# Reordering the beginning, the output projections of the last image, and the last stores of a convolution-attention kernel

## The chip, the core and the metric

The kernel runs on one core of a Trainium2 chip. A core has a matrix engine (TensorE, PE in the profile), a vector engine (VectorE, DVE), an activation engine (ScalarE, ACT), a general engine (GpSimd, POOL) and a synchronizing engine (SyncE, SP). Each takes its instructions in the order in which the program gives them to it. SP, ACT and POOL also issue DMA transfers from their queues. The metric is the device time of one execution in microseconds (us); the time before is the median of five runs.

## The reference

The input x is (4 images, 384 channels, 48 x 48). Cut to what matters:

```python
local = conv7x7_depthwise(x, conv_w)                # one 7x7 filter per channel
local = local * inv + (bn_beta - bn_mean * inv)     # inv = bn_gamma * rsqrt(bn_var + eps)
x_norm = layernorm(x_flat)                          # over the 384 channels, per pixel
q, k, v = split(x_norm @ qkv_w.T + qkv_b)           # 8 heads of 48
q = q + layernorm(local_flat)
attn = softmax((q @ k.T) * 48 ** -0.5)              # per image and head, 2304 x 2304
out = x_flat + (attn @ v) @ proj_w.T + proj_b
```

## The kernel before

**Tiles.** Channels lie on the partitions, three chunks of 128. Pixels are worked in groups of 384 (8 rows of 48), six per image, 24 in all; `t` counts them. For each image the keys and values of all six groups are made first (`from_x`); then the groups pass through attention, twelve slots each. A slot `s` is `scores` (12 products of keys and queries of one head pair, into PSUM, with ACT taking exponentials) followed by `weigh` of the slot before (24 matmul instructions with the values). PSUM has three places of two banks each, called the ring (`r`), one bank `m` that `bank()` hands out, and one bank `o` for the attention sums. A new `bank()` has to wait until everybody has read the old one.

**The convolution** is 49 taps x 3 chunks = 147 instructions of DVE per group, `acc += weight * shifted x` (L239 for a chunk's first tap, L243 for the others). `taps` is sorted by the row shift and then the column shift. `conv_ops` yields after each instruction, and `stream` chains all groups. For t = 0, chunk 0, the first ten taps (`PE_TAPS`) are done by PE as products with diagonal matrices (`make_diagonals` on ACT, `first_products`), added later by `add_products` (L761); `acc` of that chunk starts at zero (L229). So group 0 has 137 instructions on DVE.

**What sets the order.** PE, DVE and ACT run in the order written in the program, as do SP and POOL for the first loads. In the beginning `convolve_first(n)` places n taps by hand. In the slots a planner does it: `spare` estimates the time that DVE has in each half of a slot, `due` says that the taps of group t must be done by slot 6 of group t-1 (slot 8 of t = 0), and `plan` spreads the taps over the halves, starting from those already done. `convolve("slot", t, s, half)` takes them.

**The beginning.** The normalization of a group (`Norm`) is: mean over the channels, by PE, with a matrix of 1/384 (`mean_of` with three matmuls on the three chunks, or `sum` on DVE at L352 and L353 and then `mean`, one matmul, at L364); `centre` on DVE (L372); `squares` on ACT (L349); sum and mean again; `root` on ACT (L377 to L379); `newton` on DVE (L384 to L386); `scale` (L441). `newton` reads the bank `m` too.

The weights of the projections are scaled by the layer norm's gain on ACT: `scale_values` (L551), and `scale_rows(i, c)` (L558, L559) for keys (i = 1) and queries (i = 0). The layer norm's shift goes through the unscaled weights into a row for each of queries (0), keys (1) and values (2): `shift_rows` has PE multiply the shift with the weights, `rows_out` has ACT copy the row to SBUF and issue a DMA to DRAM (`bias`), and POOL issues four DMAs that bring it back as columns. `key_bias` (L562, L563) and `query_bias` (L567, L568) add these columns on DVE; ACT needs the sums when it moves keys and queries out of PSUM (L481, L494). The loads are on SP's queue in this order: the slab for the convolution, x of group 0, value weights, key weights, query weights, x of group 1, x of groups 2 to 5.

`from_x` yields after each pair of projections: two value blocks; the third value block and key 0; keys 1 and 2; queries 0 and 1; query 2. Of the first image all six groups are normalized in one loop, in which the norm of group g+1 is placed between the projections of group g; in the last turn it is the norm of the local values of group 0. `local_end` and `query_end` then add these to the queries.

**The outputs.** For images 0 to 2 the attention's results are kept in DRAM and projected in the next image's `from_x`. In the last image, group t-1 is projected in slots 5, 8 and 10 of group t, one chunk at a time in `m` (`output_step`), and `finish` (L700) adds bias and x on DVE and stores from SP (L703). `spare` lowers and raises the planner's time in these slots.

**The end.** `judge[0]` counts on PE the sums outside a safe range; `judge[1]` makes a flag of it on DVE (L1029, L1030). All engines load that flag (L1033) and branch (L1034): a second pass with shifted exponents would follow, and is skipped here.

Of the kernel before, what the change touches and what calls it, by code (L numbers as in the profile page):

```python
# [12 lines left out]
ALU = mybir.AluOpType  # L13
# [14 lines left out]
OUT_SLOTS = 5, 8, 10  # L28
PE_TAPS = 10

# [13 lines left out]
def unshifted_pass(  # L44
# [138 lines left out]
    load_packed(staged[1], qkv_wT[:, C : 2 * C])  # L183
    load_packed(staged[0], qkv_wT[:, 0:C])
    load_x(0, 1)
# [35 lines left out]
    def conv_ops(t):  # L221
# [9 lines left out]
        for i, tap in enumerate(taps):  # L231
            for c in range(CC) if t or i >= PE_TAPS else range(1, CC):
                part = window(slab, acc[:, c, :], g, first, end, c, tap)
                if not part:
                    continue
                src, dst = part
                weight = cw[:, c, tap : tap + 1]
                if tap == taps[0]:
                    nc.vector.tensor_scalar(  # L239
                        dst, src, weight, shift[:, c : c + 1], ALU.mult, ALU.add  # L240
                    )
                else:
                    nc.vector.scalar_tensor_tensor(dst, src, weight, dst, ALU.mult, ALU.add)  # L243
                yield
# [27 lines left out]
    def spare(t, s, half):  # L272
# [7 lines left out]
        if g:  # L280
            time -= {(2, 0): 0.7, (4, 1): 1.4}.get((s, half), 0.0)
            if b == B - 1 and s in OUT_SLOTS:
                time += -0.6 if half else 2.1
# [239 lines left out]
    def shift_rows(some):  # L523
        r = ring() if len(some) > 1 else None
        for j, i in enumerate(some):
            rows[i] = bank()[0:1, :C] if r is None else r[0:1, j, :C]
            project(
                rows[i],
                lambda c: beta[:, c : c + 1],
                lambda c: staged[i][:, c, :] if i < 2 else w_v[:, c, :],  # L530
            )
# [159 lines left out]
    def output_step(t, co):  # L691
        ao = outputs[t][0]
        m = bank()
        project(m[:, :G], lambda c: w_o[:, c, co * P : (co + 1) * P], lambda c: ao[:, c, :])
        finish(t, co, m[:, :G])

    def finish(t, co, m):
# [5 lines left out]
        nc.sync.dma_start(  # L703
# [61 lines left out]
    convolve_first(2)  # L765
    norm = Norm(xn[0, 0])
    norm.mean_of(norm.src)
    first_products(1)
    shift_rows((2, 1))
    convolve_first(4)  # L770
    norm.centre()
    norm.squares()
    columns = rows_out((1, 2))
    convolve_first(4)
    norm.mean_of(norm.buf)
    norm.root()
    shift_rows((0,))
    first_products(6)
    scale_values()
    columns_q = rows_out((0,))  # L780
    convolve_first(4)
    norm.scale(norm.newton())
    for c in range(CC):
        scale_rows(1, c)
    for g in range(NG):
# [4 lines left out]
        if g == 0:  # L790
            scale_rows(0, 0)
        convolve_first(10 if last else 4)
        if g == 0:
            add_products()
        norm = Norm(accs[0] if last else xn[0, g + 1])
        norm.sum()
        if g == 0:
            key_bias(columns)
        if last:
            next(making)  # L800
        norm.mean()
        convolve_first(3)
# [3 lines left out]
        if g == 0:  # L806
            scale_rows(0, 1)
            scale_rows(0, 2)
# [3 lines left out]
        norm.root()  # L812
        next(making)
        if g == 0:
            query_bias(columns_q)
        next(making)
        next(making, None)
        convolve_first(5 if last else 13)
        if last:
            local_end(0, norm.newton())  # L820
            query_end(0)
        else:
            norm.scale(norm.newton())
    plan(n_first - (each - PE_TAPS))

    for t in range(NT):
# [51 lines left out]
        for s in range(NSLOT):  # L878
# [47 lines left out]
            if s in OUT_SLOTS and g and not next_image:  # L926
                output_step(t - 1, OUT_SLOTS.index(s))
# [613 lines left out]
```

## Time and profile before

| | |
|---|---|
| median of five runs | 2972.28 us (2969.0 to 2972.81) |
| the profiled execution | 2969.26 us, span 2967.1 us |
| PE busy | 2942.5 us (99%) |
| DVE busy | 2308.5 us (78%) |
| ACT busy | 1562.9 us (53%) |
| first matmul starts | 10.94 us |
| first value projection starts | 32.43 us |
| scores of group 0 start | 147.39 us |
| last matmul ends | 2959.2 us |
| mean granted clock of PE | 0.998 |

How the lines are read. A timeline's line has the start in us, the duration in us, the engine, the line of the kernel, the operation, what it writes and reads (partitions x elements), how often, and in brackets how long the engine was idle before and what ended that. A matmul of float32 shows as two instructions. A queue has a `q` behind the engine's name. A line of the list of waits has the engine and line that waited, what for, the sum in us, how often, and the longest. A line of the table by stretches has the stretch, its length, the busy time and count of PE, its weight loads, DVE, ACT and POOL, then the clock granted to PE (1.00 is full), the DMA share and GB/s.

### The profile page before, as it was taken

What the parts mean: (1) busy time and instruction counts of PE and PEld (TensorE: products, weight loads), DVE (VectorE), ACT (ScalarE), POOL (GpSimd) and SP (SyncE); (2) the same over time, 40 slices, a digit from 0 to 9 for tenths busy, and PEclk for the clock granted to TensorE, in tenths of its full rate; (3) what the DMA queues carried; (4) which work ended last, traced back from release to release, by engine and by line L of the source; (5) the groups of instructions that cost most, each with busy time, mean ns of one, the idle gap of its engine ahead of it and who ended that gap; (6) DMA issues with size and microseconds to landing.
All of it is one profiled execution on the core that took longest, in us unless ns stands there. A gap on an engine that the chain in (4) does not pass through costs nothing.

```text
span 2967.1 us, 42344 instructions
## 1 busy us (share of the span) xinstructions
PE 2942.5 (99%) x15658; PEld 1358.0 (46%) x15658; DVE 2308.5 (78%) x4574; ACT 1562.9 (53%) x2365; POOL 25.0 (1%) x71
## 2 busy tenths in 40 slices
PE   8999999999999999999999999999999999999998
PEld 4544444444554444444455444444455444444443
DVE  7899999898788787877788878787778867677311
ACT  4355666565225565665523655566542465555553
POOL 2000000000000000000000000000000000000000
PEclk9999999999999999999999999999999999999999
DMA  6101111201231111111132111102113210100001
GB/s 111 31 13 25 44 39 32 43 22 33 83 86 24 29 34 30 30 35 35 24 90 74 26 36 33 33 21 43 37 38 91 50 26 16 33 27 20 17 26 30
DMA packets 102189, 116.53 MB, mean 39 GB/s; under 512 B 43330, under 2 KB 88915, under 8 KB 101972
## 3 DMA queue, kind: packets, MB, share of 16 engines
q1 hardware_dynamic: 100512, 113.56, 16.3%
q8 instruction: 125, 2.05, 0.3%
q14 instruction: 92, 0.75, 0.1%
q0 software_dynamic: 960, 0.07, 0.0%
q10 hardware_dynamic: 500, 0.11, 0.0%
HBM read 79.03 MB, written 24.09 MB: 35 GB/s over the span
## 4 chain that ended last, share of the span: by engine, by line
PE 96%; DVE 3%; DMA 0%; ACT 0%; issue 0%; ACTq 0%; SPq 0%; DVEq 0%
PE r L722 39%; PE o L737 38%; PE r L446 17%; DVE acc L243 3%; PE m L446 1%; PE m L364 0%; PE r L975 0%; DMA staged<-in_qkv_wT_dram 0%; DMA taps_in<-in_conv_w_dram 0%; DVE xn L372 0%; PE o L261 0%; DMA vec<-natural 0%; DVE sq L352 0%; DVE sq L353 0%; ACTq L165 0%
## 5 line engine op out<-in xcount | busy, mean ns | idle before, releaser
L726 ACT ACTIVATE pt<-r 128x768 f32<-128x768 f32 x1728 | 1275.9, 812 | 969.1 <-PE o L737 490.3
L243 DVE SCALAR_TENSOR_TENSOR acc<-slab,vec,acc 128x368 f32<-128x368 f32 (+5 forms) x3447 | 1747.3, 582 | 0.0
L737 PE MATMUL o<-pt,v 128*49 128x384 f32 x6912 | 1177.2, 490 | 0.1
L722 PE MATMUL r<-xn,k 48*128 48x384 f32 x5184 | 908.7, 497 | 0.0
L737 PEld LDWEIGHTS o<-pt,v 128*49 128x49 f32 x6912 | 426.7, 124 | 711.4 <-issue 664.4
L722 PEld LDWEIGHTS r<-xn,k 48*128 48x128 f32 x5184 | 438.3, 185 | 469.4 <-ACT pt L726 232.1
L722 PE MATMUL r<-qt,kt 48*128 48x384 f32 x1728 | 300.4, 494 | 0.0
L446 PE MATMUL r<-xn,w_qk 128*128 128x384 f32 x864 | 283.7, 486 | 0.0
L722 PEld LDWEIGHTS r<-qt,kt 48*128 48x128 f32 x1728 | 149.8, 185 | 150.3 <-ACT pt L726 68.8
L446 PEld LDWEIGHTS r<-xn,w_qk 128*128 128x128 f32 x864 | 164.2, 190 | 114.5
L352 DVE TENSOR_TENSOR sq<-sq 128x384 f32<-128x384 f32 x47 | 26.1, 555 | 163.6 <-ACT sq L349 163.5
L446 PE MATMUL r<-w_v,xn 128*128 128x384 f32 x432 | 144.4, 487 | 0.0
L643 DVE RECIPROCAL rd<-rd 128x24 f32<-128x24 f32 (+2 forms) x25 | 7.5, 301 | 168.6 <-DMA rd<-den 168.4
L475 ACT COPY v<-r 128x384 f32<-128x384 f32 x72 | 32.1, 481 | 200.3 <-PE r L446 200.3
L446 PEld LDWEIGHTS r<-w_v,xn 128*128 128x128 f32 x432 | 81.8, 190 | 58.2 <-issue 1.8
L700 DVE SCALAR_TENSOR_TENSOR xr<-r,pb,xr 128x384 f32<-128x384 f32 x57 | 33.3, 612 | 90.2 <-ACT xn L494 84.3
L494 ACT ACTIVATE xn<-r,qkb 128x384 f32<-128x384 f32 x72 | 41.8, 580 | 99.4 <-PE r L446 97.4
L446 PE MATMUL r<-af,w_o 128*128 128x384 f32 x270 | 89.5, 486 | 0.0
L481 ACT ACTIVATE k<-r,qkb 128x384 f32<-128x384 f32 x72 | 39.3, 580 | 57.4 <-PE r L446 57.4
L446 PEld LDWEIGHTS r<-af,w_o 128*128 128x128 f32 x270 | 51.3, 190 | 35.8
L626 ACT COPY ao<-o 49x384 f32<-49x384 f32 x141 | 66.7, 473 | 1.7
L700 DVE SCALAR_TENSOR_TENSOR xr<-m,pb,xr 128x384 f32<-128x384 f32 x15 | 9.2, 616 | 60.1 <-PE m L446 60.1
(117 smaller groups left out, 824.0 us busy)
## 6 DMA issues: line engine op xcount, KB each, us to landing
xr<-in_x_dram SPq DMA_DIRECT2D x24, 576.0 KB
out_dram<-xr SPq DMA_DIRECT2D x72, 192.0 KB
slab<-in_x_dram SPq DMA_DIRECT2D x32, 378.0 KB
xn<-in_x_dram SPq DMA_DIRECT2D x48, 216.0 KB
rb<-rden SPq DMA_DIRECT2D x48, 216.0 KB
held<-ao SPq DMA_DIRECT2D x15, 576.0 KB
af<-held SPq DMA_DIRECT2D x15, 576.0 KB
slab<-in_x_dram SPq DMA_DIRECT2D x16, 297.0 KB
```

Source lines behind the costliest of these rows:

```text
L243: nc.vector.scalar_tensor_tensor(dst, src, weight, dst, ALU.mult, ALU.add)
L352: nc.vector.tensor_add(self.buf[:, 0, :], src[:, 0, :], src[:, 1, :])
L446: nc.tensor.matmul(dst, lhsT=weights(c), rhs=src(c), start=c == 0, stop=c == CC - 1)
L475: nc.scalar.copy(v[:, blk, :, 0:HD], r[:, :C].rearrange("p (h d) -> p h d", d=HD))
L481: nc.scalar.activation(k[:, u, :], r[:, :G], AF.Identity, bias=qkb[:, 1, u : u + 1])
L494: nc.scalar.activation(src[:, i, :], q[:, :G], AF.Identity, bias=qkb[:, 0, i : i + 1])
L626: nc.scalar.copy(dst[r : r + HA], sums[r : r + HA, :G])
L643: nc.vector.reciprocal(rd, rd)
L700: nc.vector.scalar_tensor_tensor(xr[:, co, :], m, pb[:, co : co + 1], xr[:, co, :], ALU.add, ALU.add)
L722: nc.tensor.matmul(r[:, j, :G], lhsT=kk[:, blk * P : (blk + 1) * P], rhs=qq, start=True, stop=True)
L726: nc.scalar.activation(pt, r[:, :, :G], AF.Exp, scale=SCALE)
L737: nc.tensor.matmul(sums[r : r + HA, :G], lhsT=values[t // NG, kb // NB][:, kb % NB, 2 * p + j, :], rhs=pt[:, j, :], start=kb == 0, stop=kb ...
```

## The change

Four things move; no arithmetic is added or dropped.

1. The beginning. DVE's first eight instructions are now taps 10 to 17 of chunk 0, then the chunks 1 and 2 in turn, then the rest of chunk 0. The first mean of x is issued before those taps, after three products. The rows are made one at a time: values, then keys behind the mean of the squares, then queries in the first turn of the loop, behind the projection of value 2 and key 0; this last one uses bank `m`, and its copy, its DMAs and the scaling of the query weights come behind it. On SP, x of group 1 is loaded before the query weights.
2. The loop. All six turns have the same order: four taps, sum, mean, five taps, centring, three taps, sum of squares, thirteen taps (eight in the last turn), with the query projections after the scaling. In the first turn `add_products` and `key_bias` stand between the mean and the five taps. 165 taps are issued before the planner begins, where it was 150.
3. The last image's outputs. All three chunks are projected in a row in slot 5, behind the weighing and the taps of that slot's second half, into two places of the ring; the planner's estimate changes with it.
4. The end. The flag is made before the first `finish`, and the second store is issued by ACT.

```diff
-OUT_SLOTS = 5, 8, 10
+OUT_SLOT = 5
+AHEAD = 8
...
+    load_x(0, 1)
     load_packed(staged[0], qkv_wT[:, 0:C])
-    load_x(0, 1)
...
+        order = [(tap, c) for tap in taps for c in range(CC)]
+        if t == 0:
+            mine = [(tap, 0) for tap in taps[PE_TAPS:]]
+            order = mine[:AHEAD] + [o for o in order if o[1]] + mine[AHEAD:]
+        for tap, c in order:
...
-            if b == B - 1 and s in OUT_SLOTS:
-                time += -0.6 if half else 2.1
+            if b == B - 1 and s == OUT_SLOT and half:
+                time += 5.8 - 1.9
...
-    def shift_rows(some):
-        r = ring() if len(some) > 1 else None
-        for j, i in enumerate(some):
-            rows[i] = bank()[0:1, :C] if r is None else r[0:1, j, :C]
+    def shift_row(i, place):
+        rows[i] = place[0:1, :C]
...
-    def output_step(t, co):
+    def output(t):
         ao = outputs[t][0]
-        m = bank()
-        project(m[:, :G], lambda c: w_o[:, c, co * P : (co + 1) * P], lambda c: ao[:, c, :])
-        finish(t, co, m[:, :G])
-
-    def finish(t, co, m):
+        r, r2 = ring(), ring()
+        for co, m in enumerate((r[:, 0, :G], r[:, 1, :G], r2[:, 0, :G])):
+            project(m, lambda c: w_o[:, c, co * P : (co + 1) * P], lambda c: ao[:, c, :])
+            finish(t, co, m)
+
+    def finish(t, co, m, queue=nc.sync):
...
     first_products(3)
-    convolve_first(2)
     norm = Norm(xn[0, 0])
     norm.mean_of(norm.src)
-    first_products(1)
-    shift_rows((2, 1))
-    convolve_first(4)
+    convolve_first(AHEAD)
     norm.centre()
     norm.squares()
-    columns = rows_out((1, 2))
-    convolve_first(4)
+    first_products(3)
+    r = ring()
+    shift_row(2, r[:, 0, :])
+    scale_values()
+    convolve_first(12)
     norm.mean_of(norm.buf)
     norm.root()
-    shift_rows((0,))
-    first_products(6)
-    scale_values()
-    columns_q = rows_out((0,))
-    convolve_first(4)
-    norm.scale(norm.newton())
+    shift_row(1, r[:, 1, :])
+    first_products(4)
+    columns = rows_out((1, 2))
     for c in range(CC):
         scale_rows(1, c)
+    norm.scale(norm.newton())
     for g in range(NG):
         last = g == NG - 1
         making = from_x(0, g)
         next(making)
-        if g == 0:
-            scale_rows(0, 0)
-        convolve_first(10 if last else 4)
+        convolve_first(4)
+        norm = Norm(accs[0] if last else xn[0, g + 1])
+        norm.sum()
+        norm.mean()
         if g == 0:
             add_products()
-        norm = Norm(accs[0] if last else xn[0, g + 1])
-        norm.sum()
-        if g == 0:
             key_bias(columns)
-        if last:
-            next(making)
-        norm.mean()
-        convolve_first(3)
+        convolve_first(5)
         norm.centre()
         norm.squares()
         next(making)
         if g == 0:
-            scale_rows(0, 1)
-            scale_rows(0, 2)
+            shift_row(0, bank())
+            columns = rows_out((0,))
         convolve_first(3)
         norm.sum_squares()
         norm.mean()
         norm.root()
+        if g == 0:
+            for c in range(CC):
+                scale_rows(0, c)
         next(making)
-        if g == 0:
-            query_bias(columns_q)
-        next(making)
-        next(making, None)
-        convolve_first(5 if last else 13)
+        convolve_first(8 if last else 13)
         if last:
             local_end(0, norm.newton())
-            query_end(0)
         else:
             norm.scale(norm.newton())
+        if g == 0:
+            query_bias(columns)
+        next(making)
+        next(making)
+    query_end(0)
...
-            if s in OUT_SLOTS and g and not next_image:
-                output_step(t - 1, OUT_SLOTS.index(s))
...
             convolve("slot", t, s, 1)
+            if s == OUT_SLOT and g and not next_image:
+                output(t - 1)
...
+    judge[1]()
     finish(NT - 1, 0, parts[0])
-    judge[1]()
-    finish(NT - 1, 1, parts[1])
+    finish(NT - 1, 1, parts[1], nc.scalar)
     finish(NT - 1, 2, parts[2])
```

## The prediction

> **What bounds the kernel now.** I read the page's busy shares first, then the list of what TensorE (PE) waited for, then the timelines of PE, VectorE (DVE), ScalarE (ACT) and the queues in the first 60 us, around 217 us, in the last image and at the end.
>
> ```profile
> PE 2942.5 (99%) x15658; PEld 1358.0 (46%) x15658; DVE 2308.5 (78%) x4574; ACT 1562.9 (53%) x2365; POOL 25.0 (1%) x71
> ```
> PE works for 2942.5 of 2967.1 us. Its 24.6 us of idle time, plus time in which it runs slowly, are all that a change of order can win. The waits of PE say where they are:
>
> ```profile
> PE o L261 <- ACT pt L251: 10.9, 1, 10.9
> PE m L446 <- DVE sq L384: 2.5, 1, 2.5
> PE m L364 <- DVE sq L353: 2.5, 4, 1.7
> PE r L446 <- DMA staged<-in_qkv_wT_dram: 0.3, 1, 0.3
> ```
> The first 10.9 us are the way to the first weights, which the change leaves alone. The last matmul ends at 2959.2, about 7.9 us before the span does. Between them lie three places. Place 1 is the query row, held back until DVE has read the one bank `m`:
>
> ```profile
> 26.70 2.10 PE L446 MATMUL m<-staged,vec 128*1 128x384 f32 x6 [2.49 <-DVE sq L384]
> 32.43 4.03 PE L446 MATMUL r<-w_v,xn 128*128 128x384 f32 x12
> ```
> Place 2 is the first mean of local values in group 0, for which DVE's taps are late:
>
> ```profile
> 218.43 0.91 PE L364 MATMUL m<-sq,mean_w 128*128 128x384 f32 x2 [1.66 <-DVE sq L353]
> 219.28 5.77 PE L737 MATMUL o<-pt,v 128*49 128x384 f32 x24
> ...
> 229.14 4.08 PE L737 MATMUL o<-pt,v 128*49 128x384 f32 x24
> ```
> Behind the stall the same 24 matmuls take 5.77 us, not 4.08. The stretches of that time show why: the granted clock (the column after POOL) falls to half.
>
> ```profile
> 219.00:221.00 2.00, 2.00 (x10) 0.72 (x10) 2.00 (x5) 0.52 (x1) 0.00 (x0) 0.69 1.06 200
> 221.00:223.00 2.00, 2.00 (x10) 0.68 (x8) 2.00 (x4) 1.10 (x2) 0.00 (x0) 0.50 1.04 174
> ```
> Place 3 is the last image, where each output projection stands alone between scores and weighing:
>
> ```profile
> 2466.09 4.21 PE L722 MATMUL r<-xn,k 48*128 48x384 f32 x24
> 2470.23 2.20 PE L446 MATMUL m<-ao,w_o 128*128 128x384 f32 x6
> 2472.36 4.08 PE L737 MATMUL o<-pt,v 128*49 128x384 f32 x24
> ```
>
> **Part 1, the beginning.** No matmul goes or comes, so the question is what PE waits for. Times from the span's start. The way to 14.89 stays (three products at the slow initial pace). Then: mean of x, to 16.9; three products at 0.65, 18.9; value row 2.0, 20.8; mean of squares 2.0, 22.8; key row 2.0, 24.85; four products 2.6, 27.4. DVE does its eight taps (0.52 each, 34.37 row: 1.50 for three) from about 10.5 to 14.7, waits, centres at 17.05 to 18.4 (before: 17.99), squares end on ACT at 19.6, twelve taps end at 24.5. ACT: value weights 20.9 to 22.5 (1.61), root 22.9 to 24.65 (0.58+0.52+0.52 with starts). Newton and scale, 3.2 us (26.03 to 29.23 before), end at 27.85. The first value projection starts at 27.9, not 32.43: a gain of 4.5, of which 2.1 are only the query row, moved behind. The net 2.4 is the idle time taken out (0.32+2.49, less 0.5 that PE waits for the scale).
>
> Now what is queued behind `key_bias` on DVE. Its columns go through DRAM, and this path starts later:
>
> ```profile
> 22.11 0.88 ACT L539 COPY row<-r 1x384 f32<-1x384 f32 x2 [1.58 <-PE r L446]
> 23.03 0.49 ACTq L544 DMA_DIRECT2D bias<-row  x1
> 27.11 2.19 POOL L98 DMA_DIRECT2D columns<-bias  x4 [6.83 <-DMA bias<-row]
> 34.23 0.15 DVE L562 TENSOR_TENSOR qkb<-qk_vec,columns 128x3 f32<-128x3 f32 x1
> ```
> The fourth of POOL's issues, at 28.75, took 4.0 to land, so row issue to columns is 9.7 us, and before they were there (32.75) when DVE came (34.23). Now the key row ends at 24.85, the copies take 0.92, the issue is at 25.8 and the columns land at 35.5. DVE comes after four taps (2.1), the sum (1.1) and the added products (0.6) at 31.6: a new wait of 3.9. Behind it stand five taps (2.55) and the centring (1.3), which frees bank `m` at 39.7. PE has done values, mean, value 2 and key 0 (27.9+3.9+0.7+3.9) at 36.4 and wants that bank for the moved query row: idle 3.3. The row ends at 41.75; ACT (squares, two copies, row copy) frees `m` at 42.3, DVE's sums are ready then too, and the mean of squares starts at 42.3, where before it was 41.17: +1.1. The row before the stall of 217 us says that 1.66 us of idling cost the clock as well (5.77-4.08 = 1.7); the 2.49 us at 24 us did not (the next 2.10 is full speed). I take a slow stretch, partly under waits: +1.1 more; bounds 0 and 1.7.
>
> The query row's own chain: row copy 0.47, ACT issue 0.22, four POOL issues and a landing, 10.0 us in all (29.33 to 39.3 before), so columns at 52 to 53.5, where DVE arrives at 51.9: up to 1.6 of wait. Its twelve weight scalings (3.3) now follow the root, to 48.3 to 49.5, and query 0 needs the last third of them at 48.5 to 49.7: at nothing. SP: x of group 1 is issued four DMAs (about 2 us) earlier, the query weights as much later, wanted only at 39.7; the later x tiles are behind the bias row as before (SP waited 3.8 and 3.9 for it). From 42.3 DVE then needs thirteen taps 6.45, newton and scale 3.15, the wait 0.5, bias and four taps 2.3, sum 1.1, five taps 2.45, centring 1.3, three taps 1.5, sums 1.1: group 1's mean of squares starts at 62.1, 1.9 late (60.22 before), and 3.0 late with the slow clock. In later groups five taps instead of three add 1.0 on DVE before the centring; DVE waited 1.6, 2.0 and 2.0 there, so they are covered, in group 1 (0.98) just. If that cover were gone, each group would lose up to 1.0. Part 1: **+2.7**, the 3.0 less what PE's own small waits of the later groups before (0.1 to 0.3 each) give back; bounds -2.4 (DVE doesn't wait, the net gain above) and +4.5 (1.7 of clock, and 1.0 in one group).
>
> A page would price the wait otherwise. "DMA: Bandwidth & Descriptors" of the Trainium skill, section Anatomy of one DMA, gives about 2.0 us fixed for a small DMA. By that, as an estimate, the two hops save 3.5 and Part 1 would be about -1.6; the trace has 3.5 to 4.2 for each hop, and I go by it.
>
> **Part 2, group 0.** 165 taps are issued in the beginning, not 150. The planner's formula, worked out for both starts (13 and 28 done), gives slots 0 to 7 126 taps instead of 134. At 0.515 (69.0 us for 134) that is 64.9, and 1.1 for the sum. The query end is at DVE about 1.6 us before scores begin (before: 0.8 after), as eight taps, newton and two ends fit into five projections. So the sum is ready 64.4 us after scores begin, PE asks at 69.4 (216.77-147.39). The stall goes, and with it the slow clock: -1.66-1.7 = **-3.35**; bounds -3.4 and 0. Late next is nothing that I find: the second mean has 2 us more than it used. The Trainium skill, "TensorE: Matmul & The Clock Gate", HAM oscillation, warns only of idle gaps above about 3.4 us; by that this gap costs no clock, and Part 2 would be -1.66. The rows at 0.50 decide.
>
> **Part 3, outputs.** Alone, a projection takes 2.13 (2470.23 to 2472.36), three 6.39. Eighteen in a row behind weighing take 5.9 (742.16 to 748.07). Saved: 0.45 in each of five groups, **-2.2**; bounds -2.7 and 0. The cover: two of three ring buffers are held until `finish`. DVE sat idle 6.97 before its output at 2472.47, and the six extra taps take 3.2 of it; then finish 2 ends 0.7 before scores want its buffer. Without that cover the loss is what DVE is late, per group. The sum behind moves 7 us, but waits for ACT's squares two slots on anyway (5.83).
>
> **Part 4, the end.** The flag's two instructions (0.33) go into DVE's 1.52 of idling, the last finish and its issue come 0.3 earlier; ACT takes one issue. PE's branch (4.6 us) starts up to 1.3 earlier, SP's 0.35: **-0.5**; bounds -1.3 and 0.
>
> **Sum.** +2.7-3.35-2.2-0.5 = -3.4 (rounded). The profiled execution took 2969.26 us, 2.2 beyond its span; it would take 2965.9. The median of the runs, 2972.28, is 3.0 above it, so the forecast is 2968.9. A measurement here tells about 0.2% (5.9 us) from no change, so this is no change. Its own range is 2966 (Part 1 at 1.0, the others at their lower bounds: -6.4) to 2973 (Part 1 at 4.5, Part 3 at half: -0.4, and one more for the others).
>
> **Rivals.** *The beginning wins* (0.20): the row's path is shorter and DVE doesn't wait. For it: the wait hangs on one path of 9.7 us. Against: every hop measured 3.5 or more. Price -2.4 in Part 1, in all -8.5: 2963.8. *The stall in group 0 stays* (0.10), because query end is late: then -0.1 in all, 2972.2. Against: 5 us of margin. *ACT is held at its row issue* (0.10, slower): SP waited 3.8 for ACT's bias row, so the two queues wait for each other's transfers, and the reverse can hold ACT before the root. It decides from 3.4 us on; the x loads took 18.6 us on SP, so a hold of 10 is possible: +6.6, 2978.9. Against: neither issue waited before. The forecast has 0.55, other things 0.05.
>
> **How the numbers follow.** Faster by over 0.2%: the first rival and the forecast's edge, 0.25. Slower: most of the ACT rival, 0.10. Rest 0.65. The range takes in the first rival below; above, the stall's rival with Part 1 at +4.5 and Part 3 at 0 (-0.1+1.8+2.2 = +3.9): 2963 to 2976. That leaves out the ACT rival and little else.
>
> **What would show it.** Right: value projections at 28; DVE waiting about 4 at `key_bias` on columns; PE waiting about 3 at the query row; no wait at 217 and no half clock there; output runs of 5.9. Wrong: columns before 32, a wait of ACT at the row issue, scores in the last image waiting for DVE's `finish`.

## The result and the profile after

The changed kernel takes 2975.91 us (median of 29 runs, 2970.9 to 2979.24); the kernel before took 2970.67 us in the runs beside it (median of 49). The ratio is **1.0018, 95% interval 1.0013 to 1.0023**: slower by some 5.2 us, about the 0.2% that the prediction called its limit of measurement, and on the other side of no change than the forecast's centre (2968.9, a gain of 3.4). The profiled execution took 2975.06 us with a span of 2972.9; before, 2969.26 and 2967.1.

The busy shares of the page after say that the work is the same; PE's busy time grew by 1.2 us in 5.8 of the span.

```profile
PE 2943.7 (99%) x15658; PEld 1358.0 (46%) x15658; DVE 2312.4 (78%) x4574; ACT 1564.0 (53%) x2365; POOL 25.1 (1%) x71
```

What PE waited for, after (sum in us, how often, the longest):

```profile
PE o L265 <- ACT pt L255: 11.1, 1, 11.1
PE r L450 <- DVE xr L703: 3.6, 5, 0.7
PE m L450 <- DVE xn L376: 3.3, 1, 3.3
PE m L368 <- DVE sq L357: 1.9, 4, 1.3
PE r L450 <- DVE xn L445: 0.6, 1, 0.6
PE m L368 <- ACT row L541: 0.6, 1, 0.6
```

The old waits of 2.5 (`m`, on newton) and 1.7 us (`sq`, in group 0) are gone. In their place stand one of 3.3 us (`m`, held by the centring at L376), which the prediction had, and two that it had not: five of 0.7 us at `xr`, the output of the last image, and 1.3 us at a sum of squares.

To place the difference I cut both spans at the same landmarks in PE's timeline: the first scores of group 0, of image 1 and of image 3 (counted from 0, so image 3 is the last), and PE's last matmul.

| stretch, us | before | after | difference | forecast |
|---|---|---|---|---|
| start to the first scores of group 0 | 147.39 | 152.62 | **+5.23** | +2.7 |
| from there to the scores of image 1 | 734.29 | 730.69 | **-3.60** | -3.35 |
| images 1 and 2 | 1449.97 | 1451.49 | **+1.52** | 0 |
| last image, to PE's last matmul | 627.53 | 630.25 | **+2.72** | -2.2 |
| PE's last matmul to the span's end | 7.92 | 7.85 | -0.07 | -0.5 |
| span | 2967.1 | 2972.9 | +5.8 | -3.4 |

Place 1, the query row, in PE's timeline after:

```profile
29.05 4.11 PE L450 MATMUL r<-w_v,xn 128*128 128x384 f32 x12 [0.59 <-DVE xn L445]
...
40.98 3.45 PE L450 MATMUL m<-staged,vec 128*1 128x384 f32 x6 [3.31 <-DVE xn L376]
44.99 0.91 PE L368 MATMUL m<-sq,mean_w 128*128 128x384 f32 x2 [0.56 <-ACT row L541]
```

The first value projection comes at 29.05 (32.43 before), but the row that was moved behind it waits 3.31 us and then runs for 3.45 where it took 2.10. The mean of squares behind it starts at 44.99; it was 41.17. Place 2, the first mean of local values in group 0, has no wait any more, and the 24 matmuls behind it run at 4.08, not 5.77:

```profile
217.59 4.21 PE L725 MATMUL r<-xn,k 48*128 48x384 f32 x24
221.72 0.91 PE L368 MATMUL m<-sq,mean_w 128*128 128x384 f32 x2
222.56 4.08 PE L740 MATMUL o<-pt,v 128*49 128x384 f32 x24
```

Place 3, the outputs in a row: the three projections do not stand in one piece. A wait on `finish` (0.71 us here) parts the first from the second.

```profile
2477.38 2.20 PE L450 MATMUL r<-ao,w_o 128*128 128x384 f32 x6
2480.29 4.14 PE L450 MATMUL r<-ao,w_o 128*128 128x384 f32 x12 [0.71 <-DVE xr L703]
2484.36 4.21 PE L725 MATMUL r<-xn,k 48*128 48x384 f32 x24
```

### The profile page after: what moved, and what is told of

It is laid out like the page before. It is cut to its first block, busy times and chain, and to the rows that moved or that the text cites. A ratio compares the mean times of both kernels' runs of the same rounds, so it can differ in the third digit from the quotient of the medians.

```text
span 2972.9 us, 42346 instructions
## 1 busy us (share of the span) xinstructions
PE 2943.7 (99%) x15658; PEld 1358.0 (46%) x15658; DVE 2312.4 (78%) x4574; ACT 1564.0 (53%) x2365; POOL 25.1 (1%) x71
## 4 chain that ended last, share of the span: by engine, by line
PE 97%; DVE 2%; DMA 0%; issue 0%; ACT 0%; POOL 0%; ACTq 0%; DVEq 0%; POOLq 0%
PE r L725 40%; PE o L740 39%; PE r L450 17%; DVE acc L247 1%; PE m L450 0%; PE m L368 0%; DMA columns<-bias 0%; PE r L974 0%; PE o L265 0%; DVE xn L376 0%; DMA taps_in<-in_conv_w_dram 0%; DVE xr L703 0%; DVE sq L357 0%; DVE sq L356 0%; DVE xn L445 0%
## 5 line engine op out<-in xcount | busy, mean ns | idle before, releaser
L247 DVE SCALAR_TENSOR_TENSOR acc<-slab,vec,acc 128x368 f32<-128x368 f32 (+7 forms) x3447 | 1749.6, 582 | 4.7 <-DMA xn<-in_x_dram 3.6
L703 DVE SCALAR_TENSOR_TENSOR xr<-r,pb,xr 128x384 f32<-128x384 f32 x72 | 42.5, 613 | 156.3 <-ACT xn L498 85.6
L450 PE MATMUL r<-ao,w_o 128*128 128x384 f32 x144 | 49.6, 493 | 3.6 <-DVE xr L703 3.6
```

What stands on the lines that cost most here:

```text
L450: nc.tensor.matmul(dst, lhsT=weights(c), rhs=src(c), start=c == 0, stop=c == CC - 1)
L703: nc.vector.scalar_tensor_tensor(xr[:, co, :], m, pb[:, co : co + 1], xr[:, co, :], ALU.add, ALU.add)
```

## The experiments

All are edits of the changed kernel, and the differences below are against it unless something else is said. Eight were timed beside the kernel before; three were single runs, read by their profiles. Medians of two batches are not set against each other: the ratios are to the kernel before in the same batch.

| run | median, us (runs) | before beside it | ratio, 95% interval |
|---|---|---|---|
| outputs as before | 2973.55 (11) | 2971.49 | 1.0009 (1.0000 to 1.0018) |
| places taken in turn | 2972.35 (11) | 2971.49 | 1.0003 (0.9994 to 1.0012) |
| all projections, then all finishes | 2971.3 (11) | 2971.49 | 0.9999 (0.9990 to 1.0008) |
| key bias later | 2969.94 (11) | 2971.49 | 0.9998 (0.9989 to 1.0007) |
| query row in the ring | 2975.14 (10) | 2970.88 | 1.0015 (1.0006 to 1.0025) |
| fewer taps | 2978.54 (9) | 2970.88 | 1.0025 (1.0015 to 1.0035) |
| taps in order | 2975.17 (11) | 2970.88 | 1.0010 (1.0001 to 1.0020) |
| three edits together | 2963.7 (10) | 2970.88 | **0.9974 (0.9965 to 0.9984)** |

One figure is needed to read the beginnings: five profiles of kernels with the very same beginning (the changed kernel, the first three of the table and the one with the old end) have their first scores at 152.62, 154.22, 152.78, 153.61 and 154.59. They span 2.0 us, so a difference of up to 2 us there between single profiles is noise; +5.23 is the lowest that these five would give.

### The last image: is it the new order, or where the products land?

My theory was that the second projection waits because it shares a place of the ring with the first: a place has two banks, `r[:, 0]` and `r[:, 1]`, and the second product into it waits until `finish` has read the first. The rival was that a row of three projections is too much for the ring, or bad at that point altogether. The old outputs were put back first, with the planner's old estimate for them:

```diff
-            if s == OUT_SLOT and g and not next_image:
-                output(t - 1)
+            if s in OUT_SLOTS and g and not next_image:
+                output_step(t - 1, OUT_SLOTS.index(s))
...
+    def output_step(t, co):
+        ao = outputs[t][0]
+        m = bank()
...
```

> The changed kernel with only the outputs of the last image as before: one chunk in each of slots 5, 8 and 10, in bank m. Theory: the row of three costs time, because its second projection waits 0.71 us for the first finish, five times; undone, PE's five waits go and the span from the last image's first scores to the end falls by 2.8 us: about 2973.1 us where the changed kernel takes 2975.9. Rival: the row is a gain of 2.2 us as forecast, and the loss of the last image has another cause (the place of the code, small waits); then this takes 2978.

The last image took 627.26 us to PE's last matmul: 3.0 less than the changed kernel's 630.25, and the 627.53 of before. So the outputs lose 3 us, and it is this part that loses them. Then the order was kept and only the place changed, so that the second product goes to the other place:

```diff
-        for co, m in enumerate((r[:, 0, :G], r[:, 1, :G], r2[:, 0, :G])):
+        for co, m in enumerate((r[:, 0, :G], r2[:, 0, :G], r[:, 1, :G])):
```

> The changed kernel with the row of three outputs in the places r[0], r2[0], r[1] instead of r[0], r[1], r2[0]; order of all instructions unchanged. Theory: the second projection waits since it writes the ring place of which finish 0 still reads the other half; with another place PE's wait of 0.71 us goes and the third projection finds finish 0 done. Five times 0.71 plus 0.2 of weight load: 4 us less than the changed kernel, about 2972. Rival 1: it is the order (project, finish, project) whatever the place: then the wait stays at 0.71 and the time at 2975.9. Rival 2: the wait only moves to the scores behind, which want the places back: the wait is then on the scores' first matmuls, 0.5 to 0.7 each, time about 2975.

And, with the places as they were, all three projections ahead of all three finishes:

```diff
+        places = r[:, 0, :G], r[:, 1, :G], r2[:, 0, :G]
+        for co, m in enumerate(places):
             project(m, lambda c: w_o[:, c, co * P : (co + 1) * P], lambda c: ao[:, c, :])
+        for co, m in enumerate(places):
             finish(t, co, m)
```

> The changed kernel with all three projections issued before the three finishes, in the same places. Theory: no wait between the projections, but finish 0 now comes only after the second projection; finish 2 is done 0.6 us behind the third projection, before the scores want the second place. Output row 5.9 us, 4 us less than the changed kernel in all, about 2972. Rival (ring short): the scores behind wait for finish 1 and 2, up to 1 us each, then nothing is won: 2975 to 2976.

PE's timeline with the places taken in turn:

```profile
2473.54 4.08 PE L740 MATMUL o<-pt,v 128*49 128x384 f32 x24
2477.55 6.07 PE L450 MATMUL r<-ao,w_o 128*128 128x384 f32 x18
2483.55 4.21 PE L725 MATMUL r<-xn,k 48*128 48x384 f32 x24
```

Eighteen matmuls stand in one row of 6.07 us, and the scores behind it start at once; the kernel with all projections first has the same row. The 3.6 us at `xr` are gone from both lists of waits, and the last image takes 625.35 in both: 4.90 less than the changed kernel and 2.18 less than before. That is near the gain of 2.2 which the prediction gave to this part; against the old outputs in the otherwise changed kernel (627.26), the closer comparison, it is 1.91. The wait needs both the shared place and a `finish` ahead of the second product, since a change of either removes it. Both kernels measure as no change against before.

### The beginning: the key columns

My theory was that the 3.31 us at the query row are `key_bias`, which holds DVE, and with it the centring that frees bank `m`, until the columns have come through DRAM. The chain of work that ended last, after, in the beginning shows that path:

```profile
25.92 0.91 ACT row L541 x2
26.85 1.20 DMA bias<-row
28.09 0.53 issue
28.62 1.68 POOL columns L99 x3
30.30 6.10 DMA columns<-bias
36.43 0.04 issue
36.48 0.09 DVE qkb L564
```

The rival was that DVE's taps, sums and centring are late in any case. The edit moves `key_bias` behind the centring, ahead of the next `next(making)`, where ACT first needs its sums:

```diff
             add_products()
-            key_bias(columns)
         convolve_first(5)
         norm.centre()
         norm.squares()
+        if g == 0:
+            key_bias(columns)
         next(making)
```

> The changed kernel with key_bias moved on VectorE from in front of the five taps to behind the centring and the squares. Theory: the 4.0 us for which VectorE waits for the key columns is what delays the centring, through it bank m, the query row, the mean of squares and the slow clock. Moved, the centring ends at about 36.4 us instead of 40.9, PE's wait of 3.3 us at the query row is gone, the clock stays full, the mean of squares starts at 40 to 40.5 us instead of 45.0, scores of group 0 at about 147.5 instead of 152.6: 5 us less, about 2971. Rival: the beginning is late for other reasons, the query row's place behind the first keys and its own transfers; then VectorE's wait moves on and scores start at 151 or later, 2974.5 or more.

PE's timeline of that kernel:

```profile
37.33 2.10 PE L450 MATMUL m<-staged,vec 128*1 128x384 f32 x6
...
41.24 0.88 PE L368 MATMUL m<-sq,mean_w 128*128 128x384 f32 x2 [1.82 <-DVE sq L357]
```

The wait at the query row is gone and the row runs at full speed, 3.65 us earlier. Of these, PE gives 1.82 back at the mean of squares, since DVE now waits for the columns (2.31 us, at 38.23) after the centring instead of before it. The mean starts at 41.24, level with the 41.17 of before; the first scores start at 149.40, 3.2 us earlier than in the changed kernel and still 2.0 later than before. By these two profiles the columns cost the beginning about 3 of its 5.23 us. Timed, the edit is worth more: the ratio falls from 1.0018 to 0.9998, some 5.9 us, and the intervals do not overlap. The five profiles above, 152.62 to 154.59, have room for part of that.

The other way to free the row is another place for it. If only bank `m` holds it back, a place of the ring makes it free of DVE:

```diff
         if g == 0:
-            shift_row(0, bank())
+            shift_row(0, ring()[:, 0, :])
             columns = rows_out((0,))
```

> The changed kernel with the query row in a ring place instead of bank m, nothing else. Theory (VectorE's wait for the key columns is the cause, bank m only its carrier): the query row starts at 37.7 us without a wait, but the mean of squares still needs VectorE's sums, ready at 43.4, so PE's wait of 3.3 us moves behind the row, and the mean of squares starts at about 43.5 instead of 45.0; a slow stretch of the clock comes too. Scores of group 0 at about 151, total 1.5 us less than the changed kernel. Rival (bank m is the cause): with another place the wait goes altogether, the mean of squares starts by 41.5, scores at 148.5 to 149.

```profile
37.60 2.10 PE L450 MATMUL r<-staged,vec 128*1 128x384 f32 x6
43.46 1.27 PE L368 MATMUL m<-sq,mean_w 128*128 128x384 f32 x2 [3.76 <-DVE sq L357]
44.52 11.19 PE L450 MATMUL r<-xn,w_qk 128*128 128x384 f32 x30
```

The row came without a wait, but PE then stood 3.76 us at the mean of squares, for DVE, and worked slowly behind that: the 30 matmuls took 11.19 us where the changed kernel has 9.92. The first scores came at 152.69, against 152.62, so the 1.5 us expected of this edit did not come. The bank was only the place where PE met the delay; the columns in DVE's way are its cause.

### The beginning: the order and number of the taps

In turn 4 of the loop (turns counted from 0) PE waits 1.29 us for a sum of squares. In DVE's timeline after, the runs of thirteen taps that end the turns 2 and 3 differ:

```profile
82.98 5.65 DVE L247 SCALAR_TENSOR_TENSOR acc<-slab,vec,acc 128x235 f32<-128x235 f32 x13
102.11 7.71 DVE L247 SCALAR_TENSOR_TENSOR acc<-slab,vec,acc 128x360 f32<-128x360 f32 x13
```

In the first run the chunks 1 and 2 take turns; the second is chunk 0 alone, whose remaining taps stand at the end of the order. The size in a line is that of its first instruction; over the thirteen taps the mean is 287 elements in one run and 328 in the other. That is the smaller part of the difference. The list of instructions by size has this for the taps of 376 elements in the first run and in the second (how often, busy time in us, mean ns of one, idle time before it in us):

```profile
L247 DVE SCALAR_TENSOR_TENSOR acc<-slab,vec,acc 128x376 f32<-128x376 f32 x4 | 2.2, 601 | 0.0
L247 DVE SCALAR_TENSOR_TENSOR acc<-slab,vec,acc 128x376 f32<-128x376 f32 x2 | 1.2, 610 | 0.1
```

One tap lasts about as long in both. But where the chunks take turns, each tap starts 0.08 us before the one ahead of it has ended; where chunk 0 follows itself, it starts 0.04 us behind that end. From start to start this is 0.52 us against 0.65. In the first 160 us of the changed kernel's trace all 32 pairs of neighbouring taps that add to the same sums show such a gap, and none of the 124 other pairs does. Over the thirteen taps it makes about 1.5 of the 2.06 us; the sizes are the rest. That a tap has to wait for the sums that it adds to is the likely reason; the trace shows the gap and not the reason.

This edit mixes the chunks from the ninth tap on, with the same 137 taps:

```diff
-            order = mine[:AHEAD] + [o for o in order if o[1]] + mine[AHEAD:]
+            ahead = mine[:AHEAD]
+            rest = [(tap, c) for tap in taps for c in range(CC) if c or tap in taps[PE_TAPS:]]
+            order = ahead + [o for o in rest if o not in ahead]
```

> The changed kernel with only the first eight taps of chunk 0 ahead, and all others in the order of the taps over the three chunks; counts unchanged. Theory: PE's wait of 1.29 us in turn 4 comes from the order of the taps: chunk 0's windows of eight rows lie in turns 3 and 4, where thirteen taps take 7.71 us, and with the common order they take 5.7 as before, so the wait is 0.3 or less and scores start at about 151.2 instead of 152.6: 1.4 us less. Rival: it is the count (five taps instead of three), and the wait stays at 1 us or more.

```profile
104.88 5.93 DVE L249 SCALAR_TENSOR_TENSOR acc<-slab,vec,acc 128x376 f32<-128x376 f32 x13
```

The run at that place takes 5.93 us and the wait of 1.29 is gone. From the mean of squares to the first scores it takes 106.04 us, as before the change (106.22) and 1.59 less than the changed kernel (107.63). The first scores themselves came at 153.78, since PE's wait at the query row was 5.13 us in this execution (columns at 38.72). So the order costs the changed kernel about 1.5 us. (The theory had the reason in the sizes alone; this edit changes both, the sizes (308 on average) and chunk 0's row of taps.) The timed ratio, 1.0010 against 1.0018, agrees in direction, but their intervals overlap.

The number of taps was the other thing to try. 165 taps are issued before the planner, not 150, and group 0 no longer stalls; four taps fewer in five of the turns make 145:

```diff
-        convolve_first(8 if last else 13)
+        convolve_first(8 if last else 9)
```

> The changed kernel with nine instead of thirteen taps at the end of turns 0 to 4 of the first loop: 145 taps before the planner begins instead of 165. Theory: the wait of 1.66 us in group 0 went because the extra taps lie in the beginning; with 139 taps left for slots 0 to 7 (71.6 us at 0.515, 1.1 for the sum, from 1.6 before the scores on) the sum is ready 71.1 us behind the scores' start, PE asks at 69.4: a wait of 1.3 to 2 and a stretch of half clock come back there, +2 to +3.5. In turns 3 and 4 VectorE has less to do, and PE's wait of 1.3 in turn 4 goes. Rival: the wait went because the query end comes earlier, not by the taps; then no wait comes back, the total is 1.5 less than the changed kernel.

```profile
144.86 0.88 PE L368 MATMUL m<-sq,mean_w 128*128 128x384 f32 x2 [1.67 <-DVE sq L357]
...
226.02 0.91 PE L368 MATMUL m<-sq,mean_w 128*128 128x384 f32 x2 [1.50 <-DVE sq L357]
226.86 4.08 PE L740 MATMUL o<-pt,v 128*49 128x384 f32 x24
```

The stall in group 0 is back, with 1.50 us. So it is the taps done ahead of the planner that removed it, as the prediction had it. But the 24 matmuls behind it take 4.08 us: this pause cost no clock. Nor did fewer taps help the beginning: the wait in turn 4 fell to 0.44 us, but one of 1.67 appeared in the last turn, and the first scores came at 155.35.

### The end

The old end was put back: `finish` 0 ahead of the flag, and the second store on SP.

```diff
-    judge[1]()
     finish(NT - 1, 0, parts[0])
-    finish(NT - 1, 1, parts[1], nc.scalar)
+    judge[1]()
+    finish(NT - 1, 1, parts[1])
```

> The changed kernel with the end of before: the first finish ahead of the flag, the second store on SP. Theory A (my Part 4): from the last matmul's end to the span's end the changed kernel has 7.85 us, and with the old end this grows by 0.5, to about 8.35. Theory B (the end does not matter, because the loads of the flag and the branch on the engines set it): it lies within the 7.1 to 8.05 us seen over the kernels that share the new end, 7.5 to 7.9 like the 7.92 of before. All else stays: scores of group 0 near 152.6, last image 630.2.

The span was 2974.6 us and PE's last matmul ended at 2967.01, so the tail was 7.59 us; with the new end it was 7.1 to 8.05 in the other kernels. The rest of this profile is the changed kernel's (last image 630.23). The new end gains nothing that can be seen, and the 8.35 of theory A, my Part 4, did not come. A gain of 0.5 us is less than the spread of these tails, though, so one run does not rule it out.

### Images 1 and 2: where nothing was edited

The +1.52 us between the scores of image 1 and of image 3 are in the profile of every kernel told of so far (1451.49 to 1451.61). They come in single scores steps that are longer than the usual 4.14 from start to start. After the change there are nine of them in the whole run, 0.17 to 0.30 us too long; seven, 1.6 us in sum, lie in images 1 and 2, where the kernel before has none. (The expectations below list eight; the ninth is at 1637.72, 0.18 too long.) One in PE's and ACT's timelines after:

```profile
349.44 4.49 PE L725 MATMUL r<-xn,k 48*128 48x384 f32 x24
350.75 2.22 ACT L729 ACTIVATE pt<-r 128x768 f32<-128x768 f32 x3 [2.13 <-PE r L725]
```

ACT's first exponential starts 1.31 us behind the scores here. After an ordinary step it is 1.03, as a row below shows. Scores are held by these exponentials, which empty the ring. Since nearly the same steps are long in all those kernels, it had to be something that the program fixes. One theory: the place of ACT's instructions in its stream of instructions, if that is fetched in pieces; the other: data, transfers or another engine. Sixteen one-element copies on ACT in its idle time before 6.5 us shift that stream and leave the rest of the program as it is:

```diff
+    for _ in range(16):
+        nc.scalar.copy(spare_tile, eps[0:1])
```

> The changed kernel with 16 one-element copies on ACT in its idle time before 6.5 us, so that every later instruction of ACT stands 16 places further on in its stream. Theory A (the eight scores steps that are 0.17 to 0.30 us longer in the changed kernel, at 349.4, 952.6, 1034.3, 1286.6, 1376.1, 1808.8, 2142.5 and 2670.3, come from where ACT's instructions lie in its stream): the steps move, so most of those eight become ordinary (4.14 us) and others of 0.15 or more may show at other places. Theory B (they come from data or from another engine's stream): the same eight stay, shifted only by the time by which the beginning moves. Beginning: 152.6 or up to 1 later.

And the same on DVE:

```diff
+    for _ in range(16):
+        nc.vector.memset(spare_tile, 0.0)
```

> The changed kernel with 16 one-element memsets on DVE in its idle time at the start, so that every later instruction of DVE stands 16 places further on. Theory A (the long scores steps hang on DVE's stream): most of the eight of the changed kernel (349.4 to 2670.3) go or move. Theory B (ACT's stream, or something else): the same eight stay.

The step at 349.44 in the kernel with ACT's stream shifted:

```profile
349.65 4.21 PE L728 MATMUL r<-xn,k 48*128 48x384 f32 x24
350.68 2.21 ACT L732 ACTIVATE pt<-r 128x768 f32<-128x768 f32 x3 [1.86 <-PE r L728]
```

And with DVE's stream shifted:

```profile
347.44 4.49 PE L728 MATMUL r<-xn,k 48*128 48x384 f32 x24
348.74 2.21 ACT L732 ACTIVATE pt<-r 128x768 f32<-128x768 f32 x3 [2.13 <-PE r L728]
```

With ACT's stream shifted all nine steps became ordinary ones, and five others were long instead, at 414.82, 585.72, 1107.6, 1873.54 and 2749.7. Two of these, 0.39 us in sum, lie in images 1 and 2, which took 1450.33, 1.16 less (1.6 less 0.39 is 1.2). With DVE's stream shifted all nine stayed, each 1.8 to 2.0 us earlier as the whole beginning was, and images 1 and 2 took 1451.60. So the +1.52 hang on where ACT's instructions lie in its stream, which an edit of ACT's work ahead of them moves.

The traces show the period of it. Count every instruction that the trace has of ACT, its semaphore and DMA instructions too: each of the nine steps begins when 58, 60 or 62 instructions beyond a whole multiple of 128 have started, and so does each of the five after the shift. The kernel before has four such steps, at 167.83, 681.27, 2580.39 and 2754.05, at the same counts; by chance none of them lies in images 1 and 2. That ACT waits for a fetch of instructions fits with this and with the packets of an instruction queue (92 in the run): one falls within 5 us of the start of eight of the nine steps and of all five after the shift, where by chance some three in ten would, and none at 349.65, where the step had become ordinary. The fetch itself was not shown.

### The three edits together

Taps in order, all projections ahead of the finishes, and `key_bias` moved further: behind the centring, the three taps and the sum of squares.

```diff
             add_products()
-            key_bias(columns)
         convolve_first(5)
         norm.centre()
         norm.squares()
+        convolve_first(3)
+        norm.sum_squares()
+        if g == 0:
+            key_bias(columns)
         next(making)
         if g == 0:
             shift_row(0, bank())
             columns = rows_out((0,))
-        convolve_first(3)
-        norm.sum_squares()
         norm.mean()
```

> The changed kernel with all three remedies: key_bias behind the sum of squares, the taps in order, the three projections before the three finishes. Theory: mean of squares of the first turn at about 40 us, no wait above 0.4 in turns 1 to 5, scores of group 0 at about 146.6, no wait at the output rows: 2966 us, 5 us less than the kernel before and 10 less than the changed kernel. Rival: the remedies overlap or new small waits take their place, and it comes out level with the kernel before, 2970 to 2971.

What PE waits for in it:

```profile
PE o L267 <- ACT pt L257: 11.3, 1, 11.3
PE r L452 <- DVE xn L447: 0.6, 1, 0.6
PE m L370 <- ACT row L543: 0.6, 1, 0.6
PE m L370 <- DVE sq L359: 0.5, 2, 0.3
```

2963.7 us, ratio to before 0.9974 (0.9965 to 0.9984): faster than both kernels, by some 7.7 us against before. The span was 2959.1. The first scores start at 145.37 (147.39 before), the last image takes 625.35 (627.53), and DVE does not wait at `key_bias`, which it reaches at 37.76. Group 0 has no half-speed stretch here at all, not even the one that both kernels have behind the small products of one column (at 175 us before, 180 after). Images 1 and 2 keep their 1451.5.

## Why the prediction was wrong, step by step

**Part 3 failed in its sign: -2.2 forecast, +2.72 measured.** The failing step is the cover: "two of three ring buffers are held until `finish`", DVE has the time, "then finish 2 ends 0.7 before scores want its buffer". This looked for the wait at the scores behind the row, and the scores do not wait. The wait is inside the row, where the second projection writes to the place that the first `finish` still has to read: 5 x 0.71 = 3.6 us. The diff shows it, in the order `r[:, 0], r[:, 1], r2[:, 0]`. The parted row also works longer, 2.20 and 4.14 against 6.07 in one piece: 0.27, five times 1.3, so 4.9 in all against the kernels without the wait. The saving of the row itself was about right: without the wait it is 2.18 against before, 1.91 against the old outputs in the changed kernel.

**Part 1 had the right mechanism and was mis-sized: +2.7 forecast, +5.23 measured.** DVE waited 4.02 us at `key_bias` (3.9 forecast) and PE 3.31 at the query row (3.3). These were the points on which the part hung, and they held. The missing 2.5 us are terms:
- Everything came about 1 us later than the sum had it: the first value projection at 29.05 (27.9 forecast), the columns at 36.48 (35.5). The first mean, which now runs ahead of the taps, took 2.57 us on the chain, where I had put 2.0 to 2.1; its duration was 2.10 to 2.91 over the runs. PE's start was 0.19 later too. The total from row issue to columns was right (9.6, with 9.7 forecast), though not its halves: POOL's first issue came 1.8 us after the row's, 4.1 before the change, and the last transfer took 6.1, where I had 4.0.
- The query row ran at 3.45, not 2.10, so the slow clock cost 1.35, with 1.1 taken. By the mean of squares the loss was 3.82, against 2.2 forecast.
- Behind it another 1.41 came, against 0.5. The main piece is the 1.29 us of turn 4. I counted taps at one price, about 0.52, and said that the cover was "in group 1 (0.98) just" enough. Taps of one chunk in a row cost 0.12 more each, and the order of the taps makes the thirteen at the end of turn 3 cost 7.71, not some 5.7. (The eight taps at the start, chunk 0 alone too, took 4.89 where I had 4.2; DVE had to wait for the mean behind them in any case.)

**Part 2 was right: -3.35 forecast, -3.60 measured.** The stall and the slow stretch went, and fewer taps brought the stall back. Yet what I took from the old stall, that "1.66 us of idling cost the clock as well", is no rule: 1.50 us at the same place cost nothing.

**Part 4 was a gain of 0.5 that does not show.** The flag is made earlier, but ACT and SP come to their loads of it later (2966.0 and 2967.0 after, 2959.5 and 2960.9 before, with PE's end 5.85 later). The tail stays in its scatter.

**Images 1 and 2 were costed at nothing, without a word, and lost 1.52.** No dependence changed there. It was no term of the sum at all; the place of ACT's instructions made it, as the shifted stream showed.

The misses are then 2.5 + 4.9 + 1.5 + 0.4, less 0.25 in Part 2: 9.1, the way from -3.4 to +5.8. Of the rivals, "ACT held at its row issue" had the right sign, and its mechanism did not occur: ACT issued the row right behind its copies, at 26.85. The one that ought to have stood there is in Part 3: a `finish` between two projections that share a place. That the measured median still lies inside the range of 2963 to 2976, at its edge, is luck; the upper end was put together from the stall staying and Part 1 at its bound, with no loss in Part 3.

On the two rules of the Trainium skill that the prediction weighed: *DMA: Bandwidth & Descriptors*, Anatomy of one DMA, gives about 2.0 us fixed, for transfers issued by GpSimd. Of the two hops that is the columns', and there the slowest took 6.1 us, so it does not fit. The row's hop, issued by ACT, took 1.8 us in the changed kernel and 1.6 to 4.1 over the runs. Going by the trace was right in the sum. *TensorE: Matmul & The Clock Gate*, HAM oscillation, would leave the clock alone for gaps under about 3.4 us. The runs have slow stretches behind pauses of 1.66 us and of 2.89 to 3.31, and none behind one of 3.74, as the last section shows.

## What to carry to other kernels

Follow each product to the tile that it is written to, and ask who must still read another part of that tile: two banks of one tile were one place for a wait here, and three projections in a row were worth 2.2 us or cost 2.7 by the order of their places alone. Let neighbouring instructions of an engine add to different sums where they can: taps of one chunk in a row started 0.65 us apart, of two in turn 0.52. A small bias that goes through DRAM (here 9.6 us from row to column) belongs as late as its first reader allows, behind whatever frees a bank for the matrix engine. In this kernel, at 99% of one engine, the place of the instructions alone made 1.5 us in parts that nobody edited; a forecast of a few microseconds needs room for that.

## What was unexpected in the hardware

**Pauses and the half clock.** After PE had waited in the beginning, the six matmuls of the query row took 3.45 us after 3.31 of waiting (changed kernel), 4.00 after 2.96 (old end), 3.70 after 2.89 (ACT shifted), and 2.99 to 4.00 after 3.47 to 5.13 (five other runs), but 2.10, full speed, after 3.74 (DVE shifted). In PE's timeline of the latter:

```profile
40.29 2.10 PE L453 MATMUL m<-staged,vec 128*1 128x384 f32 x6 [3.74 <-DVE xn L379]
```

Of the 2.0 us by which the first scores of that kernel came earlier, 1.35 are the speed of this row and the rest its earlier start. A pause of 1.82 us was followed by no slow stretch, nor one of 1.50; the one of 1.66 before the change was. The clock also fell without any wait: in the changed kernel, behind 18 small matmuls of one column (177.21 to 179.31), 24 matmuls that mostly take 4.08 us took 5.77. In the three edits together it did not fall behind them. So the length of a pause does not decide by itself.

The clock's own record in the traces shows a beat. Apart from the one at a run's end, every stretch at half clock lasts 3.41 us, or two or three times that, and the stretches of one run begin a whole number of 3.41 us apart: 175.37 and 219.74 before, 40.34 and 180.28 after. Where the beat lies differs from run to run. Two beats of the changed kernel, and two with DVE shifted, as stretches (the clock is the column after POOL's):

```profile
36.93:40.34 3.41, 0.74 (x3) 0.12 (x1) 3.31 (x7) 0.00 (x0) 0.00 (x0) 1.00 0.01 2
40.34:43.76 3.42, 2.78 (x5) 0.60 (x6) 3.39 (x7) 2.01 (x3) 0.00 (x0) 0.50 0.00 0
...
34.90:38.32 3.42, 1.65 (x6) 0.64 (x4) 2.12 (x6) 0.00 (x0) 0.00 (x0) 1.00 0.29 45
38.32:41.73 3.41, 1.44 (x5) 0.42 (x6) 3.41 (x7) 1.46 (x3) 0.00 (x0) 1.00 0.00 0
```

Between the first matmuls and the scores of group 0 the clock fell to half behind each beat of which PE had idled 2.08 us or more, in nine kernels, and behind none with 1.99 or less. The beat at 38.32 parts the pause of 3.74 into 1.76 and 1.99. The small matmuls fit too: of their 2.17 us at least 1.76 lay within one beat in each kernel whose clock fell behind them; in the three edits together the beat parts them into 1.46 and 0.71. So how a pause falls on the beat can decide, and the same program may then lose the clock in one execution and keep it in the next. This is read from these traces and was not tested. It does not explain group 0, where 1.66 us within one beat cost the clock and 1.50 did not; that is left open.

**ACT's stream.** Sixteen idle copies at the start moved every one of nine delays of 0.17 to 0.30 us and were worth 1.16 us in images 1 and 2. The delays stand at one place in every 128 instructions, and which of these places fall on a scores step is set by the count of ACT's instructions ahead.
